# Layer 2 of a graph stack in blocks of 64 neighbours, and the hand-over to the flow layer

## The chip, the cores and the metric

The kernel runs on one core of one Trainium2 chip. The metric is the device time in microseconds, the median of several executions. All data is float32.

## The reference

Four graph layers follow each other on x of 32 batches, 512 nodes and 64 features, with one adjacency matrix adj of 512x512 for all. Each normalizes x, applies a relu, and adds its result to x:

```
for layer in (L0, L1, L2, L3):
    h = max(layernorm(x), 0)
    x = x + layer(h, adj)
L0: h @ w_self + (adj @ h) @ w_nbr + bias
L1: twice  z = relu((adj @ z) @ w_i)
L2: Wh = h @ W.T;  e = leaky_relu(e1[:, None] + e2[None, :], 0.2)
    att = softmax(e where adj > 0);  elu(att @ Wh)
L3: the flow layer: 8 heads of softmax((h_k h_k^T) * adj) @ h_k, leaky_relu,
    then one more such layer over the 8 heads put side by side
```

In layer 2, e1 and e2 are one number for each node: Wh times one half of the vector a. The change concerns layer 2, and the place where the flow layer begins.

## The kernel before

Nodes lie on the partitions, 128 at a time (C = 4 chunks). Layers 0 to 2 work on pairs of batches, M = 16 pairs, as a software pipeline. The function `slot(k)` of the stream (L837) is one turn of it: layer 0 of pair k, layer 1 of pairs k-2 and k-3, and layer 2 of pairs k-4 and k-5. The order of the calls in `slot` is the order of the instructions on TensorE (PE), VectorE (DVE) and ScalarE (ACT); each engine works through its queue in that order. There are M + 6 turns, k = 0 to 21. A few single steps stand after certain turns: weights, masks, scales, and at the end `judge_rows` and `judge`, which test whether adj has the form that the fast path needs.

Layer 2 is the class `Gat`. The softmax weight of neighbour j for node i splits into factors, so that no exponential of 512x512 is needed: a number c for each i, a number q for each neighbour j, and the weight max(c, q) times a 0/1 mask. A pair takes these steps:

- `flip` and `prepare` (turn k = pair + 4): the transposed features ht hold batch 0 of the pair on partitions 0 to 63 and batch 1 on 64 to 127. `project` with the block-diagonal weights wgT2 gives wh for both batches (L725, 4 matmuls of 128x128 with 128 columns). Four matmuls with wa2 give e2 (L747, 2 columns), and one for each batch gives e1, spread over all partitions (L753, 512 columns). ACT makes v's last column, q and c from them by exponentials.
- `weigh`: DVE scales wh by that last column.
- `scores` (turn k = pair + 5): for each batch and each chunk of 128 neighbours one DVE operation (L779) writes the weights s, 128x512.
- `values`: acc (L789) is the sum over neighbours, 4 chunks of nodes by 4 chunks of neighbours for each batch, each a matmul of a 128x128 block of s with 65 columns of v. A float32 matmul stands in the trace as two instructions, each with its weight load.
- `end`: DVE divides (L801, L802), ACT makes the exponential e of elu (L807), DVE adds to x (L810, L811) and centres x for the next normalization, ACT squares it (L813). Its variance goes into the next turn's sums (L684, L691, L699).

The mask of layer 2 is made once by one DVE operation from the transposed adjacency (L935).

The flow layer is a second schedule, `run` (L962), with a `slot(k)` of its own (L978), from k = -12. Its first unit is prepared in the first turns: DVE normalizes (L475 to L479), GpSimd scales into hs (L484), TensorE transposes into hx_ps (L291), ACT copies to hx, TensorE multiplies into g_ps (L509), ACT copies to g (L521), and then the scores s_ps (L387) begin. The PSUM buffers of this schedule (ps_s, ps_m, ps_v) take the place of those of the stream (ps_t, ps_o, ps_g), which are given back in between.

Of the kernel before, what the change touches and what calls it, by code (L numbers as in the profile page):

```python
# [22 lines left out]
def fast_form(  # L23
# [51 lines left out]
    adj_raw = setup.tile([P, C, N], F32, name="adj_raw")  # L75
# [54 lines left out]
    wgT2 = setup.tile([P, F2], F32, name="wgT2")  # L130
# [3 lines left out]
    wa2 = setup.tile([P, 2], F32, name="wa2")  # L134
# [105 lines left out]
    def gat_weights():  # L240
        pw = acc("wgT_ps", [P, F2])
        nc.tensor.transpose(pw, wg2, ident)
        nc.scalar.copy(wgT2, pw)
# [4 lines left out]
        nc.vector.memset(wa2, 0.0)  # L248
        for k in range(2):
            nc.vector.tensor_copy(wa2[halves(k), k : k + 1], wa[halves(k), 1:2])  # L250
# [207 lines left out]
    class Heads(Pair):  # L458
# [31 lines left out]
        def prep_pe(self, step):  # L490
            b, i = self.b, self.i
            if step == -1 and i == 0:
                Heads.hx[b] = pair_transpose(
                    ps_m, lambda n: wk.tile([P, N], F32, name=n), Heads.hs.pop(b), "hx",
                    nc.scalar.copy, "m",
                )
# [3 lines left out]
        def row_halves(self, off):  # L500
            b, i = self.b, self.i
            if off == -C:

                pss = [ps_m.tile([P, N], F32, name="g_ps", tag="m") for k in range(2)]
# [13 lines left out]
                for k in range(2):  # L518
                    u = self.pair[k]
                    u.g = wk.tile([P, N], F32, name="g", bufs=3)  # L520
                    nc.scalar.copy(u.g, pss[k])  # L521
# [28 lines left out]
    class Out(Pair):  # L550
# [51 lines left out]
        def end_late(self, step):  # L602
# [4 lines left out]
            elif step == 2:  # L607
                xb = row_pair("y")[:, 0].rearrange("p (k c f) -> p k c f", k=2, c=C)
                for k in range(2):
# [7 lines left out]
                    )  # L617

# [9 lines left out]
    with (  # L628
# [105 lines left out]
        class Gat:  # L734
# [8 lines left out]
            def prepare(self):  # L743
                self.wh_ps = project([(self.ht, wgT2)], "wh")
                e2 = ps_t.tile([P, C, 2], F32, name="e2_ps", tag="ps")
                for c in range(C):
                    nc.tensor.matmul(  # L747
                        e2[:, c], lhsT=self.ht[:, c * P : (c + 1) * P], rhs=wa2,
                        start=True, stop=True,
                    )  # L750
                e1 = [ps_t.tile([P, N], F32, name="e1_ps", tag="ps") for k in range(2)]
                for k in range(2):
                    nc.tensor.matmul(  # L753
                        e1[k], lhsT=wa1[halves(k), :], rhs=self.ht[halves(k), :],
                        start=True, stop=True,
                    )
                self.v = work.tile([P, 2, C, F + 1], F32, name="v")
                self.q = tiny.tile([P, C, 2], F32, name="q")
                nc.scalar.activation(
                    self.v[:, :, :, F].rearrange("p k c -> p c k"), e2, AF.Exp, scale=0.2  # L760
                )
                nc.scalar.activation(self.q, e2, AF.Exp, scale=0.8)
                self.c = row_pair("c")
                for k in range(2):
                    nc.scalar.activation(self.c[:, k], e1[k], AF.Exp, scale=-0.8)

            def weigh(self):
                nc.vector.tensor_tensor(
                    self.v[:, :, :, :F],
                    self.wh_ps.rearrange("p c k f -> p k c f"),  # L770
                    self.v[:, :, :, F : F + 1].to_broadcast([P, 2, C, F]),
                    OP.mult,
                )

            def scores(self, k):

                self.s = getattr(self, "s", []) + [[row_pair("s") for j in range(C // 2)]]
                for j in range(C):
                    nc.vector.scalar_tensor_tensor(  # L779
                        self.s[k][j // 2][:, j % 2], self.c[:, k], self.q[:, j, k : k + 1],  # L780
                        mask_t[:, j], op0=OP.max, op1=OP.mult,
                    )

            def values(self, k):
                acc = ps_g.tile([P, C, F + 1], F32, name="acc")
                self.acc = getattr(self, "acc", []) + [acc]
                for r in range(C):
                    for j in range(C):
                        nc.tensor.matmul(  # L789
                            acc[:, r],  # L790
                            lhsT=self.s[k][j // 2][:, j % 2, r * P : (r + 1) * P],
                            rhs=self.v[:, k, j],
                            start=(j == 0),
                            stop=(j == C - 1),
                        )

            def end(self):
# [8 lines left out]
                e = work.tile([P, 2, C, F], F32, name="e")  # L806
# [6 lines left out]
                nc.scalar.activation(o, o, AF.Square)  # L813

        n0, n1, n2, gat = {}, {}, {}, {}
        nt1b, z, po0 = {}, {}, {}
# [20 lines left out]
        def slot(k):  # L837
# [25 lines left out]
            u = gat.get(k - 5)  # L863
# [33 lines left out]
            if k - 6 in gat:  # L897
                some.append(gat.pop(k - 6))
# [3 lines left out]
            if u:  # L902
                u.values(0)
                u.values(1)
# [11 lines left out]
            if l1:  # L916
                nt1b[k - 2] = neighbours(lambda c: z[:, c, :])
            if u:
                u.end()

        mask_t = setup.tile([P, C, N], F32, name="mask_t")
        with tc.manual_schedule(
# [7 lines left out]
            for k in range(M + 6):  # L930
                slot(k)
                if k == 0:
                    gat_weights()
                elif k == 1:
                    nc.vector.tensor_scalar(mask_t, adj_t, 0.0, None, op0=OP.is_gt)  # L935
                elif k == 2:
                    masks()
                elif k == 3:
                    flow_weights()
                elif k == 4:  # L940
                    scales()
                elif M < k <= M + C:
                    judge_rows(k - M - 1)
                elif k == M + C + 1:
                    judge()
# [14 lines left out]


    def run(units, products):  # L962
        units = units + [None] * 4

        def at(k, off, span=C):

            for u in range(len(units)):
                if units[u] and 0 <= k - u * C - off < span:
                    yield units[u], k - u * C - off

        exps = []

        def led_in(k):
            for u, j in at(k, -3 * C, 3 * C + END + 5):
                if u.leads(j - 3 * C):
                    yield u, j - 3 * C

        def slot(k):  # L978
            for u, r in at(k, -1):
                u.scores(r)  # L980

            led = list(led_in(k))
            for u, off in led:
                u.row_halves(off)

            while exps:
                exps.pop(0)()

            copies = []

            def transposes():
                for u, j in at(k, TR):
                    copies.append(u.transpose(j))

            if not led:
                transposes()
            for u, j in at(k, VA):
                u.values(j)  # L1000
            for u, j in at(k, VA - 1, 1):
                u.make_v()
# [654 lines left out]
```

## Time and profile before

| | before |
|---|---|
| median of 3 runs | 2357.64 us (2357.25 to 2358.01) |
| profiled execution, own time | 2361.5 us |
| its span, first to last instruction | 2359.7 us |
| mean granted TensorE clock | 0.981 |
| first flow scores (s_ps) start | 480.16 us |

Layers 0 to 2 take the first fifth of the span. The page's slices are 59 us each, so they are slices 1 to 8 and a little of the ninth; the rest is the flow layer. In the timelines PE is a matmul, PEld a weight load, and a number in square brackets is the time that the engine stood idle before the row, with the instruction that ended it. Neighbouring rows of one group are merged: the length is from the start of the first to the end of the last.

### The profile page before, as it was taken

Reading aid. Unit: us, or ns where it says so; the run is one execution under the profiler, and the core shown is the slowest. Engines: PE = TensorE matmul, PEld = TensorE weight load, DVE = VectorE, ACT = ScalarE, POOL = GpSimd, SP = SyncE. Lnnn points to the kernel's source line nnn. Section 1 sums busy time; section 2 is a strip of 40 time slices with the busy share of each in tenths; the row PEclk is TensorE's granted clock in tenths of the full one; section 3 lists DMA queues with packets and bytes.
Section 4 is the critical chain, followed back from the end, with each engine's and each line's share of the span. In section 5 each row is a group of like instructions: output and inputs, shape, how many; then the busy total and the mean of one; then the engine's idle time right before and its main releaser. Section 6 shows DMA issues by size and latency. Waiting matters only on the chain.

```text
span 2359.7 us, 46961 instructions
## 1 busy us (share of the span) xinstructions
PE 2259.6 (96%) x17786; PEld 1107.3 (47%) x17786; DVE 1792.1 (76%) x4350; ACT 1583.2 (67%) x3660; POOL 68.0 (3%) x104
## 2 busy tenths in 40 slices
PE   7999999689999999999999999999999999999997
PEld 4677777634444444444444444444444444444443
DVE  5788878577777777777777777777777787878776
ACT  3444443277777777777777777777777777778775
POOL 2000000000000000000000000000000000000000
PEclk9999999589999999999999999999999999999999
DMA  3000000000000000000000000000000000000001
GB/s 106 1 1 1 1 1 1 0 15 24 20 28 21 27 24 24 28 20 28 22 26 24 24 24 24 24 24 24 24 24 26 22 29 19 24 19 24 20 24 38
DMA packets 44059, 51.89 MB, mean 22 GB/s; under 512 B 15864, under 2 KB 25248, under 8 KB 43696
## 3 DMA queue, kind: packets, MB, share of 16 engines
q1 hardware_dynamic: 43312, 48.60, 6.6%
q8 instruction: 142, 2.33, 0.4%
q0 software_dynamic: 512, 0.20, 0.1%
q14 instruction: 93, 0.76, 0.1%
HBM read 43.98 MB, written 4.78 MB: 21 GB/s over the span
## 4 chain that ended last, share of the span: by engine, by line
PE 89%; DVE 6%; POOL 2%; ACT 1%; issue 1%; DMA 1%; SPq 0%; POOLq 0%; DVEq 0%; ACTq 0%
PE s_ps L387 23%; PE av L415 22%; PE pt_ps L400 13%; PE nt_ps L706 7%; PE acc L789 6%; PE gT_ps L566 5%; PE y_ps L527 5%; PE g_ps L509 2%; DVE pt_att L408 2%; POOL hs L484 2%; PE po L725 1%; PE hx_ps L291 1%; PE e_ps L753 1%; PE po1a L725 1%; PE wh L725 1%
## 5 line engine op out<-in xcount | busy, mean ns | idle before, releaser
L366 ACT ACTIVATE p_att<-s_att,negmax 128x512 f32<-128x512 f32 x1152 | 827.6, 723 | 0.0
L373 DVE CUSTOM_DVE_ANT_0 s_att<-s_ps,flow_neg 128x512 f32<-128x512 f32 x1152 | 739.9, 680 | 5.3 <-PE s_ps L387 5.2
L408 DVE COPY pt_att<-pt_ps 128x512 f32<-128x512 f32 x576 | 395.6, 687 | 281.0 <-PE pt_ps L400 223.7
L387 PE MATMUL s_ps<-hx,g 64*128 64x512 f32 x2048 | 571.0, 636 | 5.8 <-DVE negmax L373 5.1
L415 PE MATMUL av<-pt_att,hn 128*64 128x512 f32 x2048 | 552.4, 618 | 0.0
L400 PEld LDWEIGHTS pt_ps<-ident,p_att 64*128 64x128 f32 x9216 | 373.6, 138 | 374.1 <-issue 227.7
L406 ACT COPY pt_att<-pt_ps 128x512 f32<-128x512 f32 x576 | 334.6, 581 | 156.6 <-PE pt_ps L400 150.7
L400 PE MATMUL pt_ps<-ident,p_att 64*128 64x64 f32 x9216 | 415.2, 226 | 2.3 <-ACT pt_att L406 0.8
L535 ACT ACTIVATE cat<-y_ps,bh 128x512 f32<-128x512 f32 x256 | 162.0, 684 | 168.4 <-PE y_ps L527 168.4
L387 PEld LDWEIGHTS s_ps<-hx,g 64*128 64x128 f32 x2048 | 156.5, 188 | 245.7 <-DVE negmax L373 178.3
L366 ACT ACTIVATION_READ_ACCUMULATOR p_att<-s_att,negmax 128x1 f32 x1152 | 224.5, 195 | 0.0
L444 DVE TENSOR_TENSOR o_att<-av,recb 128x512 f32<-128x512 f32 x144 | 99.6, 691 | 140.5 <-PE av L415 140.5
L415 PEld LDWEIGHTS av<-pt_att,hn 128*64 128x64 f32 x2048 | 101.4, 135 | 156.7 <-PE s_ps L387 86.4
L312 DVE SCALAR_TENSOR_TENSOR cat<-cat 128x1024 f32<-128x1024 f32 x128 | 155.6, 1215 | 0.0
L789 PE MATMUL acc<-v,s 128*128 128x65 f32 x1024 | 136.5, 301 | 10.3 <-DVE s L779 10.3
L789 PEld LDWEIGHTS acc<-v,s 128*128 128x128 f32 x1024 | 134.8, 217 | 13.5 <-issue 12.3
L527 PE MATMUL y_ps<-o_att,wh_sb 64*128 64x512 f32 x512 | 131.7, 591 | 0.0
L566 PE MATMUL gT_ps<-cat,wo_sb 128*64 128x512 f32 x512 | 131.7, 593 | 0.0
L521 ACT COPY g<-g_ps 128x512 f32<-128x512 f32 x128 | 68.7, 589 | 84.8 <-PE g_ps L509 84.8
L706 PE MATMUL nt_ps<-adj_t,hn 128*128 128x512 f32 x256 | 115.9, 596 | 0.8 <-DVE hn L670 0.8
L373 DVE DVE_READ_ACCUMULATOR2_ANT negmax<- 128x1 f32 x1152 | 95.6, 83 | 0.0
L387 PE MATMUL s_ps<-gs 64*128 64x512 f32 x256 | 72.3, 641 | 24.2 <-DVE gs L584 24.2
(169 smaller groups left out, 1603.1 us busy)
## 6 DMA issues: line engine op xcount, KB each, us to landing
recb<-rec_row SPq DMA_DIRECT2D x288, 128.0 KB
rec_row<-rect SPq DMA_DIRECT2D x576, 1.0 KB
out_dram<-y SPq DMA_DIRECT2D x32, 128.0 KB
x<-in_x_dram SPq DMA_DIRECT2D x3, 1024.0 KB
x<-in_x_dram SPq DMA_DIRECT2D x4, 256.0 KB
adj_raw<-in_adj_dram SPq DMA_DIRECT2D x1, 1024.0 KB
wh_sb<-in_L_gnn_Wh_dram SPq DMA_DIRECT2D x2, 256.0 KB
wo_sb<-in_L_gnn_W_out_dram SPq DMA_DIRECT2D x1, 256.0 KB
```

The source lines that it names most:

```text
L366: nc.scalar.activation(self.p[:, k, r, :], ns[:, k], AF.Exp, bias=self.negmax[:, k, r : r + 1], scale=-1.0, accum_out=self.sum[:, k, r : r ...
L373: nc.vector.tensor_tensor_reduce(out=ns[:, k], in0=ps[:, k], in1=flow_neg[:, r], scale=-1.0, scalar=BIG, op0=OP.add, op1=OP.min, accum_out ...
L387: nc.tensor.matmul(ps[:, k], lhsT=g[halves(k), r * P : (r + 1) * P], rhs=x[halves(k), :], start=True, stop=True,)
L400: nc.tensor.transpose(ps[half][:, k, r], self.p[halves(half), k, r, j * P : (j + 1) * P], ident[halves(half), halves(half)],)
L406: nc.scalar.copy(pth[:, :, :, 0, :], ps[0])
L408: return lambda: nc.vector.tensor_copy(pth[:, :, :, 1, :], ps[1])
L415: nc.tensor.matmul(self.av[halves(k), :], lhsT=self.v(k, j), rhs=pt[k], start=(j == 0), stop=(j == C - 1),)
L527: nc.tensor.matmul(ps, lhsT=wh_sb[halves(k), h, :], rhs=self.o[halves(k), :], start=True, stop=True,)
L535: nc.scalar.activation(self.cat[:, k], pss[k], AF.Identity, bias=bh[:, h : h + 1], scale=1.0)
L566: nc.tensor.matmul(self.gps[halves(k), :], lhsT=wo_sb[:, h, :], rhs=Heads.cat[b + k, h], start=(h == 0), stop=(h == H - 1),)
L706: nc.tensor.matmul(p, lhsT=lhs(k), rhs=adj_t[:, k, :], start=(k == 0), stop=(k == C - 1))
L789: nc.tensor.matmul(acc[:, r], lhsT=self.s[k][j // 2][:, j % 2, r * P : (r + 1) * P], rhs=self.v[:, k, j], start=(j == 0), stop=(j == C - 1),)
```

## The change

Layer 2 takes the neighbours in 8 blocks of 64 instead of 4 of 128. Both batches of a pair now share each tile: batch 0 on partitions 0 to 63, batch 1 on 64 to 127. wh and e2 come from one matmul for each block and batch, with W and its product with a side by side in wgv (65 columns); batch k uses the rows and writes the partitions of half k. c is one tile for both batches. In `values` the two batches alternate, each on its row half of TensorE, into an accumulator of its own. The mask needs both halves of the partitions for each block: four DVE operations write one half each, and four DMAs on the SP queue copy it to the other.

The last pair is scored, multiplied and ended in the turn in which it is prepared (k = 19), so there are M + 5 turns. The single steps now stand before the last part of a turn (`end`), and the judge rows come one turn earlier. The exponential e goes to a buffer of another pool. The first 11 turns of the flow schedule, up to g, run after turn k = 17 (M + 1), in the stream and with its PSUM buffers; `run` becomes `planned`, which returns its `slot`. From there on the flow schedule is as it was.

```diff
     def gat_weights():
         ...
-        nc.scalar.copy(wgT2, pw)
+        for k in range(2):
+            nc.scalar.copy(wgv[halves(k), :F], pw[halves(k), halves(k)])
         ...
-        nc.vector.memset(wa2, 0.0)
-        for k in range(2):
-            nc.vector.tensor_copy(wa2[halves(k), k : k + 1], wa[halves(k), 1:2])
+        nc.vector.tensor_copy(wgv[:, F:], wa[:, 1:2])
...
     class Gat:
             def prepare(self):
-                self.wh_ps = project([(self.ht, wgT2)], "wh")
-                e2 = ps_t.tile([P, C, 2], F32, name="e2_ps", tag="ps")
-                for c in range(C):
-                    nc.tensor.matmul(
-                        e2[:, c], lhsT=self.ht[:, c * P : (c + 1) * P], rhs=wa2,
-                        start=True, stop=True,
-                    )
-                e1 = [ps_t.tile([P, N], F32, name="e1_ps", tag="ps") for k in range(2)]
+                self.wh_ps = [
+                    ps_t.tile([P, C, F + 1], F32, name="wh_ps", tag="ps") for b in range(2)
+                ]
+                for b in range(2 * C):
+                    for k in range(2):
+                        nc.tensor.matmul(
+                            self.wh_ps[b // C][halves(k), b % C],
+                            lhsT=self.ht[halves(k), b * F : (b + 1) * F],
+                            rhs=wgv[halves(k), :], start=True, stop=True,
+                        )
+                e1 = ps_t.tile([P, N], F32, name="e1_ps", tag="ps")
                 for k in range(2):
                     nc.tensor.matmul(
-                        e1[k], lhsT=wa1[halves(k), :], rhs=self.ht[halves(k), :],
+                        e1[halves(k), :], lhsT=wa1[halves(k), :F], rhs=self.ht[halves(k), :],
                         start=True, stop=True,
                     )
...
+                for b in range(2):
+                    e2 = self.wh_ps[b][:, :, F]
+                    some = slice(b * C, (b + 1) * C)
+                    nc.scalar.activation(self.v[:, some, F], e2, AF.Exp, scale=0.2)
+                    nc.scalar.activation(self.q[:, some], e2, AF.Exp, scale=0.8)
+                self.c = row_pair("c")[:, 0]
+                nc.scalar.activation(self.c, e1, AF.Exp, scale=-0.8)
...
+            def scores(self, part):
+                self.s = getattr(self, "s", []) + [row_pair("s") for b in range(C // 2)]
+                for b in range(part * C, (part + 1) * C):
                     nc.vector.scalar_tensor_tensor(
+                        self.s[b // 2][:, b % 2], self.c, self.q[:, b : b + 1],
+                        mask_t[b // C][:, b % C], op0=OP.max, op1=OP.mult,
+                    )
...
+            def values(self):
+                self.acc = [
+                    ps_g.tile([P, C, F + 1], F32, name="acc") for k in range(2)
+                ]
                 for r in range(C):
+                    for b in range(2 * C):
+                        for k in range(2):
+                            nc.tensor.matmul(
+                                self.acc[k][:, r],
+                                lhsT=self.s[b // 2][halves(k), b % 2, r * P : (r + 1) * P],
+                                rhs=self.v[halves(k), b],
+                                start=(b == 0), stop=(b == 2 * C - 1),
+                            )
...
-                e = work.tile([P, 2, C, F], F32, name="e")
+                e = row_pair("e")[:, 0].rearrange("p (k c f) -> p k c f", k=2, c=C)
...
-        def slot(k):
+        def slot(k, more):
...
+            if more:
+                more()
+            last = gat.pop(M - 1) if k - 4 == M - 1 else None
+            if last:
+                last.scores(0)
+                last.scores(1)
             if u:
                 u.end()
+            if last:
+                last.values()
+                last.end()
...
+        def edges():
+            for b in range(2):
+                for k in range(2):
+                    blocks = mask_t[b][:, k::2]
+                    nc.vector.tensor_scalar(
+                        blocks[halves(k)], adj_t[halves(k), b * C // 2 : (b + 1) * C // 2],
+                        0.0, None, op0=OP.is_gt,
+                    )
+                    nc.sync.dma_start(blocks[halves(1 - k)], blocks[halves(k)])
...
             start()
-            for k in range(M + 6):
-                slot(k)
...
+            begun = {
+                0: gat_weights,
+                1: edges,
+                2: masks,
+                3: flow_weights,
+                4: scales,
+                M + 4: judge,
+            }
+            for c in range(C):
+                begun[M + c] = lambda c=c: judge_rows(c)
+            for k in range(M + 5):
+                slot(k, begun.get(k))
+                if k == M + 1:
+                    for i in range(-3 * C, -1):
+                        flow_slot(i)
...
+        for k in range(-1, (len(flow) + 4) * C):
+            flow_slot(k)
```

## The prediction, made before the changed kernel ran

> **What bounds the kernel now.** I read the page first: busy shares, slices, clock.
>
> ```profile
> span 2359.7 us, 46961 instructions
> ...
> PE 2259.6 (96%) x17786; PEld 1107.3 (47%) x17786; DVE 1792.1 (76%) x4350; ACT 1583.2 (67%) x3660; POOL 68.0 (3%) x104
> ...
> PEclk9999999589999999999999999999999999999999
> ```
>
> TensorE is busy 96% of the time, but the clock row has a dip at slices 8 and 9, about 400 to 490 us. That is where layers 0 to 2 end and the flow layer begins. The change touches only what stands before the first flow scores (s_ps, 480.16 us): in the built programs the instructions from s_ps on are the same on PE, DVE and ACT. So the question is when the first s_ps starts.
>
> Next the chain of waits in order of time, for one slot out of the middle:
>
> ```profile
> 121.15 7.09 PE acc L789 x64
> 128.24 1.84 PE po L725 x16
> 130.08 6.87 PE nt_ps L706 x16
> 136.95 0.44 PE ht_ps L291 x4
> 137.38 0.89 PE po1b L725 x8
> 138.28 0.44 PE ht_ps L291 x4
> 138.71 3.44 PE nt_ps L706 x8
> 142.15 0.89 PE wh L725 x8
> 143.04 0.79 PE e_ps L747 x8
> 143.83 1.06 PE e_ps L753 x4
> 144.89 1.09 PE po1a L725 x8
> ```
>
> The pieces follow without a gap: a slot is 24.83 us of TensorE and nothing else (DVE is busy 21.1 of it, ACT 10.7). A cheaper DVE or ACT step is worth nothing here; only these rows count. Last the TensorE timeline where the pairs run out (columns: start, length, instructions, idle before and its releaser):
>
> ```profile
> 404.17 12.47 PE L789 MATMUL acc<-v,s 128*128 128x65 f32 x58 [0.23 <-DVE s L779]
> 422.94 2.08 PE L725 MATMUL wh<-wgT,ht 128*128 128x128 f32 x8 [5.46 <-ACT ht L293]
> 428.46 13.92 PE L789 MATMUL acc<-v,s 128*128 128x65 f32 x64
> 452.26 14.53 PE L789 MATMUL acc<-v,s 128*128 128x65 f32 x64 [9.88 <-DVE s L779]
> 477.11 0.37 PE L223 MATMUL own_ps<-ident,own 128*1 128x128 f32 x1 [8.41 <-DVE own L221]
> 480.16 6.78 PE L387 MATMUL s_ps<-hx,g 64*128 64x512 f32 x16 [0.67 <-ACT g L521]
> ```
>
> Here TensorE waits for DVE and ACT, and an acc block takes 14 us instead of 7.1, since the granted clock is 0.50 (windows of 404 to 477 us). It does not come back during 20 us of unbroken work (422.9 to 442.4), only after the dense s_ps run.
>
> **What a half-height weight load costs.** Blocks of 64 neighbours double the matmuls of acc (512 to 1024 per layer; two instructions each), half of them on each row half. The rate is set by weight loads, so I took the load rows of the timeline:
>
> ```profile
> 96.04 4.32 PEld L789 LDWEIGHTS acc<-v,s 128*128 128x128 f32 x38
> 904.75 0.30 PEld L387 LDWEIGHTS s_ps<-hx,g 64*128 64x128 f32 x4
> 906.49 0.20 PEld L415 LDWEIGHTS av<-pt_att,hn 128*64 128x64 f32 x4
> ```
>
> acc: (4.32 - 0.192) / 37 = 0.112 us per 128-column load. s_ps, row halves: four loads of 0.188 within 0.30, so two start together and the next two about 0.11 later. A half-height load of 128 columns takes as long as a full one, and the halves load side by side. av: 64 columns, (0.20 - 0.135) = 0.065 to the second pair, half of it.
>
> **The steady slot, part by part.**
> acc: 64 pairs of instructions at 0.110 to 0.116 = 7.0 to 7.4 us against 7.09: no gain in itself.
> wh and e2 (L747): 8 + 8 full loads, 0.89 + 0.79 = 1.68, become 16 pairs of 64-column loads with 65 columns streamed: about 0.06 each = 0.96. Gain 0.7.
> e1 (L753): its two matmuls already run side by side (4 instructions of 0.43 us streaming in 1.06); they still do. 0.
> Changes of array shape: each costs about 0.2 (po1a after e1: 1.09 for a block that is 0.89 elsewhere). Before there are two in a slot (into e1, out of it), after four (wh, po1a, acc, po). Loss 0.4.
> Sum per slot: -0.35, between -0.6 and -0.1. Slots 4 to 15 are TensorE-bound: 12 x 0.35 = 4.2 us.
>
> At nothing: one c exponential less, four small ones of 128x4 for two of 128x8 on ACT (10.7 of 24.8 busy); weigh as two operations (+0.1 on DVE); both accumulators now finish together, so end's first half starts 3.5 us later and ends 0.65 later. The second scores have 2.4 us of slack before acc (342.03 against 344.47); without it, acc would stop at its first row block, which now needs all eight score blocks. The mask becomes four operations on 64 partitions, about 2.5 us for 1.22; DVE idles 3.53 us at 39.81 and absorbs it. Its four 256 KB copies wait on SP behind the x loads; DMA traffic is down to 2 GB/s by 30 us, nothing else stands in that queue until 493 us, and the mask is first read at 85 us: 45 us of cover for an estimated 5. The gat_weights step loses two copies and a memset on DVE and gains an ACT copy: 0.2 less of a 1.5 us wait.
>
> **The place where a rule of the skill speaks against it.** No row of the trace has two row halves writing into one PSUM bank: s_ps, y_ps and g_ps give each half a tile of its own, and av puts two column halves into one bank (loads 6 ns apart in the 0.20 us row). In the new wh and e1, half k reads rows k and writes partitions k of one tile. The Trainium skill, TensorEngine Tiling (Array Packing), Restrictions and Gotchas, says that different row tiles cannot access the same PSUM bank simultaneously. By that rule wh takes 32 x 0.06 = 1.9 and e1 1.9 instead of 1.0: +1.8 per slot, so 1.4 slower instead of 0.35 faster. I go by the av row: there, too, two tiles share the bank but not the partitions.
>
> **The tail, step by step** (times on the clock of before; slot k is the k-th turn of the stream).
> Slot 16: judge_rows(0) moves in front of end: +4.0 us on DVE (447.35 to 451.37 is one). The second scores end at 386.9 instead of 386.1; acc(12) still ends at about 392.4.
> Slot 17: DVE goes on at 386.9 with var, weigh, relu (3.0), judge (4.0), end (4.3: the exp table load of 1.28 no longer waits behind o, since e now has another buffer), then the flow preparation hn (1.3; before it stands at 107.8, in slot 6): 399.6. POOL makes hs (1.2): 400.4. In TensorE's queue hx_ps stands next after nt of z, which ends at 396.1: 4.3 us idle. So the clock halves here, as it did at 404.
> Slot 18: hx 0.9, copy 0.6, g_ps 1.9, two g copies on ACT to 405.2; only then, in ACT's order, nt1b (405.7) and ht (406.3). Behind them po1b (to 407.6), DVE's addition, centring and second scores (412.6), wh and e1 on TensorE (411.6). acc(13) runs 411.9 to 426.1: 9.5 later than before (416.6).
> Slot 19: end 4.3, square and ht copy 1.3, wh and e1 at half clock 4.1: acc(14) 435.8 to 449.9. Meanwhile DVE does the last pair's scores (to 446.7), so acc(15) follows without the 9.88 us wait: 449.9 to 464.0.
> Slot 20: end 4.3, square 0.7, table load 1.3, root, rstd, own, own_ps 1.3: s_ps at about 471.7, since the judge rows (4.4) and g (3.0) are out of the way. Before, acc end to s_ps was 13.4; now 7.6.
> Tail: 471.7 - 480.16 = -8.4 us; the flow preparation costs 9.5 of a gain of 18.
>
> Sum: -4.2 - 8.4 - 0.2 = -12.8, less about 0.5 for a later return of the clock: -12.3. The profiled execution (span 2359.7, own time 2361.5) gives a span of 2347.4; its own time is 3.9 over the median 2357.64. From the median: 2345.3.
>
> **Rivals.**
> A. As summed, 2345, +-6 for the sizes of the slot and of some ten tail steps: 0.70.
> B. The clock stays full in the tail. Then acc(13) ends at 416, acc(14) at 432, acc(15) at 442, s_ps at 450: 30 us instead of 8.4, 2324; a halving one slot later gives some 2335. For it: blocks at half use kept the clock in the steady slots. Against it: 4.3 us idle where 2.38 and a few stalls were enough before. 0.10.
> C. Slower: the two row halves wait for each other at the shared bank. +1.8 on 12 steady slots, the same in 16 and 17, double at half clock in 18 and 19: 1.8 x 18 = +32, so 2377. It decides from 12.5 / 18 = 0.7 us per slot on. Against it: av; for it: the rule. 0.12, from 2358 on.
> D. The flow preparation costs the tail all it gains (hs or the ACT copies later still, another 8 us): only the steady gain is left, 2353. That is also the case where the change doesn't do what it says: the last pair has no slot, but its work waits as long. 0.08.
>
> **How the numbers follow.** This kernel's runs lie within 0.03%; 0.2% (4.7 us) is what can be told from no change. Faster, below 2352.9: nearly all of A, B and a third of D: 0.82. Same: rest of D, edges of A and C: 0.06. Slower: C: 0.12. Range 2331 to 2354: A, half of B, half of D; C and the full-clock end of B stay out.
>
> **What would show it.** Steady slot about 24.5 us, acc still near 7.1, wh about 1.0 with no e2. Clock 0.50 from about 400 until shortly after s_ps. The hx_ps row with some 4 us idle before it, released by POOL hs; two acc blocks back to back of 14 us each; s_ps at about 467 on the new clock. A slot over 25 us with wh near 1.9 shows C; acc of 7 us in the tail shows B. A mask wait (DMA) before the first scores, or any difference after s_ps, would make the sum wrong in a way not foreseen.

## Result and profile after

| | before | after |
|---|---|---|
| median (seven runs each, same session) | 2360.4 us (2357.25 to 2361.58) | 2341.07 us (2338.13 to 2351.17) |
| ratio, 95% interval | | 0.9933 (0.9914 to 0.9952) |
| profiled execution, own time | 2361.5 us | 2340.76 us |
| its span | 2359.7 us | 2338.9 us |
| first acc block starts | 96.15 us | 94.47 us |
| acc(12) ends (nt of z starts) | 392.23 us | 386.66 us |
| first flow scores start | 480.16 us | 459.83 us |

(acc(i) is the acc block of pair i; there are 16.) The changed kernel is faster by 0.7%, inside the range and 4 us below the point forecast. "The tail" below is the stretch from the end of acc(12) to the start of s_ps. Of the 20.8 us that the span lost, 20.3 are gone by the first flow scores: 5.6 before acc(12) ends, 14.8 in the tail. The page of the profile after:

```profile
span 2338.9 us, 49561 instructions
...
PE 2248.0 (96%) x19066; PEld 1086.8 (46%) x19066; DVE 1794.3 (77%) x4366; ACT 1576.3 (67%) x3674; POOL 68.4 (3%) x104
...
PEclk9999999599999999999999999999999999999999
```

There are more instructions and TensorE is busy for less time; the dip in the clock row is now one slice wide instead of two. A steady turn, from the TensorE timeline of after (start, length, instructions):

```profile
143.22 7.36 PE L924 MATMUL acc<-v,s 64*128 64x65 f32 x128
150.51 0.49 PE L852 MATMUL po<-ws,ht 128*128 128x128 f32 x2
...
152.40 3.60 PE L833 MATMUL nt_ps<-adj_t,z 128*128 128x512 f32 x8
...
161.04 3.60 PE L833 MATMUL nt_ps<-adj_t,hn 128*128 128x512 f32 x8
164.57 1.15 PE L878 MATMUL wh_ps<-wgv,ht 64*64 64x65 f32 x32
165.55 1.03 PE L885 MATMUL e_ps<-ht,wa 64*64 64x512 f32 x4
166.51 1.16 PE L852 MATMUL po1a<-wl,nt 128*128 128x128 f32 x8
```

The next acc starts at 167.59: a turn of 24.37 us instead of 24.83, still without a gap. The tail, same view:

```profile
394.53 1.03 PE L290 MATMUL hx_ps<-ident,hs 128*128 128x128 f32 x4 [4.17 <-POOL hs L483]
405.28 7.71 PE L924 MATMUL acc<-v,s 64*128 64x65 f32 x128
423.12 13.92 PE L924 MATMUL acc<-v,s 64*128 64x65 f32 x128
437.85 14.43 PE L924 MATMUL acc<-v,s 64*128 64x65 f32 x128 [0.82 <-DVE rec L935]
459.00 0.37 PE L223 MATMUL own_ps<-ident,own 128*1 128x128 f32 x1 [6.72 <-DVE own L221]
459.83 4.61 PE L386 MATMUL s_ps<-hx,g 64*128 64x512 f32 x12 [0.46 <-DVE unsound L224]
```

acc(13) takes 7.71 us, the other two 14: the clock halved at the hx wait as forecast, but came back for that one block. The stretches of the tail (length, busy time of TensorE, weight loads, VectorE, ScalarE and GpSimd with instructions, granted clock):

```profile
396.00:406.00 10.00, 9.17 (x65) 5.76 (x66) 4.17 (x9) 3.72 (x11) 0.00 (x0) 0.56 0.01 2
406.00:416.00 10.00, 7.45 (x124) 7.00 (x122) 9.59 (x21) 3.50 (x4) 0.00 (x0) 0.96 0.01 2
416.00:426.00 10.00, 6.52 (x64) 4.91 (x64) 9.18 (x17) 4.30 (x10) 0.00 (x0) 0.50 0.00 0
```

The seven runs show that this is not fixed: two took 2350.2 and 2351.2 us at a mean clock of 0.980 and 0.979, the other five 2338 to 2344 at 0.985 to 0.988. One acc block more at half clock would be 7 us of the 9 to 10 that part these two from the profiled run; neither of the two has a profile, so this is an estimate.

### The profile page after: what moved, and what is told of

Its sections match the earlier page's. It is cut to its first block, busy times and chain, and to the rows that moved or that the text cites. A ratio compares the mean times of both kernels' runs of the same rounds, so it can differ in the third digit from the quotient of the medians.

```text
span 2338.9 us, 49561 instructions
## 1 busy us (share of the span) xinstructions
PE 2248.0 (96%) x19066; PEld 1086.8 (46%) x19066; DVE 1794.3 (77%) x4366; ACT 1576.3 (67%) x3674; POOL 68.4 (3%) x104
## 4 chain that ended last, share of the span: by engine, by line
PE 72%; DVE 4%; POOL 2%; issue 1%; ACT 0%; DMA 0%; SPq 0%; POOLq 0%; DVEq 0%
PE s_ps L386 23%; PE av L414 23%; PE pt_ps L399 13%; PE y_ps L526 5%; PE gT_ps L565 5%; PE g_ps L508 2%; DVE pt_att L407 2%; POOL hs L483 2%; PE hx_ps L290 1%; DVE hn L475 1%; DVE s_att L372 1%; DVE hn L474 0%; DVE gs L583 0%; PE gV_ps L576 0%; PE back_ps L449 0%
## 5 line engine op out<-in xcount | busy, mean ns | idle before, releaser
L924 PE MATMUL acc<-v,s 64*128 64x65 f32 x2048 | 132.5, 291 | 1.5 <-DVE rec L935 0.8
L924 PEld LDWEIGHTS acc<-v,s 64*128 64x128 f32 x2048 | 129.5, 206 | 6.9 <-issue 2.6
```

Of the source, the lines that this page charges most:

```text
L924: nc.tensor.matmul(self.acc[k][:, r], lhsT=self.s[b // 2][halves(k), b % 2, r * P : (r + 1) * P], rhs=self.v[halves(k), b], start=(b == 0) ...
```

## Experiments

Twelve kernels, the changed one again among them, each stand beside runs of the kernel before on the same chip. The rows come from four chips, on which the kernel before had medians of 2358.0 to 2359.2 us. The intervals are 0.07 to 0.2% of a ratio to either side, so that 2 or 3 us between two rows are not told from nothing. "Half" names the acc blocks of the tail that ran wholly or partly at half clock in the profiled execution, whose own time stands beside it.

| kernel | median us (runs) | ratio to before, 95% | profiled: us, s_ps start, half |
|---|---|---|---|
| 64-blocks only | 2355.66 (12) | 0.9984 (0.9975 to 0.9992) | 2356.11, 476.31, acc 13 14 15 |
| judge rows only | 2359.55 (22) | 0.9993 (0.9986 to 1.0) | 2352.17, 470.99, 14 15 |
| own turn for the last pair | 2336.18 (4) | 0.9908 (0.9892 to 0.9925) | 2336.63, 454.30, 15 (13 for 0.7 us) |
| no preparation in the stream | 2336.48 (4) | 0.9895 (0.9881 to 0.9909) | 2336.72, 457.09, 13 14 15 |
| after, again | 2341.97 (5) | 0.9919 (0.9906 to 0.9932) | 2338.04, 457.28, 15 |
| preparation in turns 8 to 10 | 2336.38 (4) | 0.9900 (0.9886 to 0.9914) | 2336.66, 455.84, 13 15 |
| after + dense matmuls | 2341.43 (6) | 0.9927 (0.9907 to 0.9947) | 2337.08, 458.74, 15 |
| judge rows in turns 5 to 12 | 2329.83 (4) | 0.9867 (0.9849 to 0.9885) | 2337.02, 457.02, 13 14 15 |
| tail reordered | 2333.71 (4) | 0.9896 (0.9880 to 0.9913) | 2333.37, 452.65, 14 15 |
| both | 2328.49 (4) | 0.9870 (0.9854 to 0.9887) | 2332.61, 452.97, 13 14 15 |
| both + 7 dense steps | 2325.09 (4) | 0.9854 (0.9840 to 0.9868) | 2325.00, 443.86, 15 |
| both + 16 dense steps | 2318.07 (5) | 0.9826 (0.9813 to 0.9840) | 2318.68, 437.63, none |

### The 64-blocks alone

```diff
-            for k in range(M + 5):
-                slot(k, begun.get(k))
-                if k == M + 1:
-                    for i in range(-3 * C, -1):
-                        flow_slot(i)
+            for k in range(M + 6):
+                slot(k)
+                if k in begun:
+                    begun[k]()
...
```

The lines left out take the last pair's steps out of `slot` and put the judge rows back behind `end`, in turns M + 1 to M + 4.

> Only the first half of the change: blocks of 64 neighbours, wgv, the mask in two tiles and e in a row tile, but 22 turns of the stream as before, the last pair in its own turn, the judge rows and the judge where they were, and the flow preparation after the stream. Account theory: the gain ahead of the tail comes with these parts, 1.7 us before the first acc block and 0.41 us in each of 12 turns, 6.6 us; in the tail the table load that no longer waits behind o gives some 1.3 us in each of three turns, and both accumulators ending together take back 0.6 in each: about 9 us under the kernel before. Rival (the whole gain lies in the reordered tail): within 2 us of the kernel before. Rival (the two row halves wait for each other): 20 us over it.

Measured: 3 us under before, between the theories. From its first acc block to the end of acc(12) it does gain 4.6 us (291.51 against 296.08). (Two spells of half clock in its first 86 us, which the profiles of before and after do not have, hide the start.) But its tail, from acc(12)'s end to s_ps, is 88.2 us against 87.9: all that the earlier table load should give is gone. TensorE and VectorE timelines of this kernel:

```profile
397.40 1.01 PE L924 MATMUL acc<-v,s 64*128 64x65 f32 x8 [0.48 <-DVE s L911]
...
402.27 12.92 PE L924 MATMUL acc<-v,s 64*128 64x65 f32 x112 [2.31 <-DVE s L911]
```

```profile
396.51 2.73 DVE L911 SCALAR_TENSOR_TENSOR s<-c,q,mask 128x512 f32<-128x512 f32 x4
...
401.48 2.73 DVE L911 SCALAR_TENSOR_TENSOR s<-c,q,mask 128x512 f32<-128x512 f32 x4
```

acc(13) stops in its first row block for the second half of the scores (begun at 401.48), and the clock halves at 399.4. The scores end 4.9 us earlier than before (404.2 against 409.1), the block only 1.5 (415.2 against 416.6). With blocks of 128 neighbours the first batch of the pair could be multiplied before the scores of the second were there; blocks of 64 need all eight scores in each block of rows.

### The judge rows alone

```diff
+            if more:
+                more()               # judge_rows(k - M), ahead of u.end()
             if u:
                 u.end()
...
-                elif M < k <= M + C:
-                    judge_rows(k - M - 1)
```

> The kernel before, with one edit: each of the four judge rows comes a turn earlier and ahead of end instead of behind it, as in the changed kernel; blocks of 128 neighbours, the last pair's own turn and the flow preparation after the stream stay. Theory (the place of the judge rows carries what the tail gains: 4.0 us of VectorE leave the way from end to the next scores and the way to own_ps, which is what 64-block half alone, 2355.7, lacks to 2336.2): 13 to 19 us under the kernel before, 2340 to 2345. Rival (the place of the rows helps only with blocks of 64 or with the clock that came back by chance): within 6 us of the kernel before.

Measured: no difference in the median. The runs fall into two groups: 16 at 2359.0 to 2362.0 us with clock 0.980 or 0.981, and 6 at 2352.2 to 2353.3 with 0.985. The profiled one is of the second group:

```profile
405.59 7.36 PE L789 MATMUL acc<-v,s 128*128 128x65 f32 x64
...
425.91 13.92 PE L789 MATMUL acc<-v,s 128*128 128x65 f32 x64
...
445.69 14.53 PE L789 MATMUL acc<-v,s 128*128 128x65 f32 x64 [5.87 <-ACT o L813]
```

acc(13) met the full clock, and 7 us is what one acc block at half clock costs. The rival holds for the median: the moved rows pay nothing in most runs. That the slower group had acc(13) at half clock is likely from its mean clock, but none of it was profiled.

### The last pair in a turn of its own

```diff
-            last = gat.pop(M - 1) if k - 4 == M - 1 else None
-            if last:
-                last.scores(0)
-                last.scores(1)
             if u:
                 u.end()
-            if last:
-                last.values()
-                last.end()
...
-                if k == M + 1:
-                    for i in range(-3 * C, -1):
-                        flow_slot(i)
```

> The changed kernel without the preparation in the stream (2336.5 in the run before) and with the last pair in a turn of its own again; the judge rows stay where the change puts them. It stands between the 64-block half alone (2355.7) and 2336.5, and tells what the merged last turn is worth by itself. Account theory: the last acc block waits again for end of the pair ahead of it (4.3 us) and its own eight scores (5.4 us), 9 us instead of 0.8: about 2345, so the merged turn gives 9 and the place of the judge rows the other 10. Rival (the place of the judge rows does it all): 2339 or less. Rival (the merged turn does it all): 2353 or more.

The last lines take the preparation out of the stream as well. Measured: 2336.18, as fast as the kernel without preparation that merges the last turn (2336.48). The merge shows no gain, though the two profiles met different clocks, and the rival that the judge rows do it all holds: 19.5 us below the 64-blocks alone. Its timelines, TensorE and VectorE:

```profile
398.11 7.90 PE L924 MATMUL acc<-v,s 64*128 64x65 f32 x128
...
416.04 7.36 PE L924 MATMUL acc<-v,s 64*128 64x65 f32 x128
428.60 15.48 PE L924 MATMUL acc<-v,s 64*128 64x65 f32 x128 [5.20 <-ACT o L947]
```

```profile
384.17 0.42 DVE L195 TENSOR_SCALAR edge<-adj_p 128x512 f32<-128x512 f32 x1
...
388.19 0.17 DVE L935 RECIPROCAL rec<-acc 128x4 f32<-128x4 f32 x1
...
397.43 2.73 DVE L911 SCALAR_TENSOR_TENSOR s<-c,q,mask 128x512 f32<-128x512 f32 x4
```

A judge row stands in the time in which VectorE would wait for acc(12) (384.2 to 388.2, acc ends at 387.2), instead of between end and the scores; the second scores of pair 13 start at 397.43 instead of 401.48, acc(13) runs unbroken, at full clock from 398.8 on, and ends at 406 instead of 415. From there the clock does the rest: acc(14) and acc(15) with the wait between them take 416.04 to 444.08, 28.0 us, where the 64-blocks alone took 40.1 (424.48 to 464.61). In that kernel both ran at half clock and here only acc(15), so part of the 19.5 us is the clock; how much of it the place of the rows would give at one clock was not measured.

### No preparation in the stream, and the changed kernel again

```diff
-                if k == M + 1:
-                    for i in range(-3 * C, -1):
-                        flow_slot(i)
...
-        for k in range(-1, (len(flow) + 4) * C):
+        for k in range(-3 * C, (len(flow) + 4) * C):
```

> The changed kernel, but the first flow unit is not prepared in the stream: it comes after the stream, as before. Account theory (the preparation delays acc of the third last pair by the wait for hs, hx, g and the ACT copies): that block starts some 6 us earlier, and hx and g find room in the wait before own_ps; 3 to 7 us under the changed kernel if the clock behaves alike, so 2334 to 2338. Rival (the preparation is worth having, because it takes hx and g off the way to s_ps): 3 us or more over the changed kernel. Rival (the clock decides): the time goes with the granted clock of the tail, not with the waits, and the seven or so runs fall into clusters some 9 us apart.

> The changed kernel once more, on the same chip as the other two, to place it against the kernels that leave the preparation out (2336.2 to 2336.5). If the preparation in the stream costs the 5 us that separate runs suggest: 2339 to 2345, above every one of those runs. If the difference was the chip or the day: 2335 to 2338.

Measured: 2336.48 without it; the changed kernel came out at 2341.97, all five of its runs above every one of the four (on another chip, with the kernel before at 2359.2 there and 2358.9 here). The preparation in the stream costs about 5 us. The timeline without it:

```profile
400.71 8.67 PE L924 MATMUL acc<-v,s 64*128 64x65 f32 x100 [0.22 <-DVE s L911]
...
418.66 13.92 PE L924 MATMUL acc<-v,s 64*128 64x65 f32 x128
433.40 14.43 PE L924 MATMUL acc<-v,s 64*128 64x65 f32 x128 [0.82 <-DVE rec L935]
448.81 1.09 PE L290 MATMUL hx_ps<-ident,hs 128*128 128x128 f32 x4 [0.98 <-DVE o L936]
```

acc(13) starts 8 us earlier (397.31) and ends at 409.3 instead of 413.0, although the clock halved in it; hx and g lie in the wait before own_ps. acc(14) and acc(15) take 418.66 to 447.83 here, 29.2 us with no wait between them, against the 28.0 with the wait of 5.2 in the kernel above. So the merge takes out a wait, but in this execution it got both blocks at half clock.

### The preparation earlier

```diff
-                if k == M + 1:
-                    for i in range(-3 * C, -1):
-                        flow_slot(i)
+                for i in {8: range(-12, -5), 9: range(-5, -4), 10: range(-4, -1)}.get(k, ()):
+                    flow_slot(i)
```

> The changed kernel with the preparation of the first flow unit moved from the tail to turns 8, 9 and 10 of the stream: hn and hs in 8, hx in 9, g in 10. It costs about 1.9 us of TensorE there, which is the bound, and takes the wait of 4.2 us for hs, hx, the wait for its copy and g (6.5 us in all) out of the tail. Account theory: 2 to 5 us under the changed kernel, 2336 to 2339, if the clock of the tail stays as it is. Rival (the third last acc block then meets the half clock, since the wait that leads up to it goes on elsewhere): within 2 us of 2341 or slower.

Measured: 2336.38, as expected, and the same as without preparation. acc(12) ends at 388.13, 1.5 later than in the changed kernel; the tail is 5.5 us shorter (67.7 against 73.2). In the profiled run acc(13) did meet the half clock, as the rival has it, but acc(14) had the full one.

### Dense matmuls in the waits of the changed kernel

```diff
+        def warm(n):
+            p = ps_o.tile([P, N], F32, name="warm", tag="po")
+            for j in range(n):
+                nc.tensor.matmul(
+                    p, lhsT=ident, rhs=adj_t[:, j % C, :], start=(j == 0), stop=(j == n - 1)
+                )
...
```

> The changed kernel with 18 extra matmuls of 128x128 by 512 that nothing reads: 5 before hx_ps, 6 before wh of the second last pair, 7 before own_ps, each group put where TensorE waited 4 to 7 us for others. Clock theory (TensorE's half clock in the tail is what the two last acc blocks of 14 us cost): the clock stays full up to s_ps, the acc blocks take 7.3 us, s_ps comes about 14 us earlier, 2327 in all, and the runs lie within 2 us of each other. Rival (the clock in the tail is not the limit, the chain through VectorE and ScalarE is): within 2 us of the changed kernel's 2341. Rival (the extra work is in the way): slower than 2341.

Measured: the median did not move, and the runs spread over 16 us, with the clock: 2333.85 at 0.993, 2349.78 at 0.986. The clock theory as put failed. The profiled run shows why full clock in two of the blocks did not help more:

```profile
423.83 5.80 PE L924 MATMUL acc<-v,s 64*128 64x65 f32 x100 [0.22 <-DVE s L911]
435.12 14.43 PE L924 MATMUL acc<-v,s 64*128 64x65 f32 x128 [5.49 <-DVE rec L935]
```

acc(14) is done at 429.6, 7.4 us earlier than in after (9.9 if counted from the end of acc(12), which came 2.5 us later in this execution). But VectorE still has a judge row and the last eight scores ahead of end, until 434.3, so acc(15) waits 5.5 us, meets the half clock again and starts only 2.7 us earlier. VectorE had to come first.

### Less VectorE in the tail, and another order

In the first kernel the judge rows are cut in two and put into turns 5 to 12 (its lines shift by 6); in a second kernel two steps are moved; a third has both edits. The first two:

```diff
-            for c in range(C):
-                begun[M + c] = lambda c=c: judge_rows(c)
+            for c in range(2 * C):
+                begun[5 + c] = lambda c=c: judge_rows(c // 2, c % 2)
...
```

```diff
+            if k == M + 2:           # ahead of end of pair 13
+                gat[M - 1] = Gat(M - 1, n2.pop(M - 1).h)
+                gat[M - 1].flip()
+                gat[M - 2].scores(0)
+                gat[M - 2].scores(1)
...
```

> The changed kernel without the preparation in the stream, with the four judge rows (4.0 us of VectorE each) cut in halves of 2 us and put into turns 5 to 12, where VectorE waits some 4.4 us a turn. Theory (in the tail TensorE waits for VectorE, and that wait brings the half clock): the scores of the third last pair come 4 us sooner, its acc block is done at 405 instead of 410 us, 1 to 4 us less in all, 2333 to 2336. Rival (the order of the tail, not the load of VectorE, sets its end: the rows stand in waits for acc): within 1 us of 2336.5. Rival (TensorE-bound turns lose by it): slower than 2336.5 by up to 2.

> The changed kernel without the preparation in the stream, with two steps moved: the transposition of the last pair's input, and the scores of the second last pair, come ahead of end of the third last pair instead of behind it. Theory (the second last acc block waits for end of the block before it only by the order on ScalarE and VectorE): the wait of 4.6 us for ht goes and acc follows wh at once; s_ps 9 us sooner, about 2328 at half clock, less where the clock stays full. Rival (VectorE is the limit whatever the order, since it has judge, end and scores to do between two acc blocks): within 3 us of 2336.5.

> Both of the last two kernels' edits: judge rows in turns 5 to 12, and the last pair's transposition and the second last pair's scores ahead of end of the third last pair. Theory (with neither the order nor VectorE in the way TensorE has hardly a wait, so its clock stays full up to the last acc block): from the end of the third last acc block to s_ps 27 to 30 us instead of 47, about 2315. Rival (the clock drops all the same): the gain of the order alone and 2 us more, about 2326.

Measured: 2329.83, 2333.71 and 2328.49 (all three without preparation in the stream). Judge rows out of the tail gave more than expected in the median, but with runs of 2322.62 at clock 0.992 and 2337.02 at 0.985, and the slowest is the profiled one; the order gave 2.8, its rival's figure and not clear of noise; both gave 8 and stand near the rival's 2326, the clock having dropped all the same. In the reordered kernel the wait for ht is 0.73 us instead of 4.6, and VectorE is late next:

```profile
412.16 14.43 PE L924 MATMUL acc<-v,s 64*128 64x65 f32 x128 [3.64 <-DVE rec L935]
```

### The clock held

The kernel with both edits gets dense steps in its own short waits: first 7, then, in a second kernel, 16.

```diff
             if last:
+                warm(1)              # second kernel: warm(6)
                 last.values()
...
-                M + 4: judge,
+                M + 4: lambda: (warm(4), judge()),      # second kernel only
```

The other six steps are 2 ahead of po1b and 3 ahead of acc(13) in turn 18, and 1 ahead of wh in turn 19.

> The kernel with judge rows in turns 5 to 12 and the reordered tail (2328.5), plus 7 dense matmul steps of 128x128 by 512 that nothing reads (0.86 us each at full clock): 2 ahead of po1b and 3 ahead of acc of the third last pair, 1 ahead of wh and 1 ahead of the very last acc block, where TensorE waited 1.6, 1.2, 0.7 and 0.8 us. Clock theory (a few short waits are enough to halve the clock at about 399 us, and the halved clock then costs 7 us in each of the last two acc blocks): the clock stays full until after the last acc block, s_ps about 13 us earlier, 2315. Rival (the clock drops in spite of it, since blocks of 65 columns use half the array at most): 2327 to 2331. Rival (VectorE is the limit behind it): 2322 to 2326.

> The kernel at 2325.1 with more of the dense matmuls that nothing reads: 6 instead of 1 ahead of the very last acc block, where TensorE still waited 4.3 us for VectorE and the clock halved, and 4 between that block and hx. Clock theory (each acc block at half clock costs 7.1 us, and this is the last one left): that block takes 7.3 us instead of 14.4, s_ps comes 7 us earlier and its first twelve matmuls take 2.6 us instead of 4.9: 2316 to 2319. Rival (the last block was off the path that sets the end, or the clock drops all the same): within 2 us of 2325.

Measured: 2325.09, then 2318.07. In the first, acc(15) still waited 4.27 us and took 14.43; VectorE was late. In the second, the TensorE timeline and the stretches of the tail:

```profile
396.91 7.36 PE L930 MATMUL acc<-v,s 64*128 64x65 f32 x128
...
407.59 7.36 PE L930 MATMUL acc<-v,s 64*128 64x65 f32 x128
414.88 5.42 PE L982 MATMUL warm<-adj_t,ident 128*128 128x512 f32 x12
420.26 7.88 PE L930 MATMUL acc<-v,s 64*128 64x65 f32 x128
...
437.63 4.58 PE L392 MATMUL s_ps<-hx,g 64*128 64x512 f32 x12 [0.46 <-DVE unsound L230]
```

```profile
406.00:416.00 10.00, 10.00 (x163) 8.64 (x160) 6.82 (x15) 4.87 (x10) 0.00 (x0) 1.00 0.01 2
416.00:426.00 10.00, 9.86 (x107) 7.08 (x105) 7.52 (x15) 2.54 (x3) 0.00 (x0) 1.00 0.01 2
426.00:436.00 10.00, 7.52 (x54) 4.15 (x51) 5.33 (x11) 3.40 (x5) 0.00 (x0) 1.00 0.00 0
```

acc(15) starts at the same time in both (420.16 and 420.26); only its clock differs, 14.43 against 7.88 us, 6.55 of the 7.0 us that the second kernel gains in the median: the price of one block at half clock, measured. The four steps behind it gained nothing: from acc(15)'s end to s_ps it is 9.5 us, against 9.3. The clock then halved at 437.8, as s_ps began, and its first twelve instructions took 4.58 us, not the 2.6 expected. All five runs lie within 1.4 us. This kernel beats both the kernel before (0.9826) and the changed one; it spends 16 steps of TensorE on nothing but its clock.

## Why the prediction was right, and where its steps were not

**Steady slot, forecast -0.35, measured -0.46.** From the start of one row to the start of the next: wh and e2 1.77 to 0.98, -0.79 (forecast -0.7); e1 1.06 to 0.96, -0.10 (0); acc 7.10 to 7.29, +0.19 (0); into wh +0.09, po1a to acc +0.09, po +0.05. The sum is -0.47. The rows of before, to set beside those of after:

```profile
141.99 1.05 PE L725 MATMUL wh<-wgT,ht 128*128 128x128 f32 x8
142.88 0.95 PE L747 MATMUL e_ps<-wa,ht 128*128 128x2 f32 x8
143.76 1.13 PE L753 MATMUL e_ps<-ht,wa 64*128 64x512 f32 x4
144.82 1.16 PE L725 MATMUL po1a<-wl,nt 128*128 128x128 f32 x8
145.81 7.26 PE L789 MATMUL acc<-v,s 128*128 128x65 f32 x64
```

The mis-sized term is the change of array shape: forecast +0.4 for the two additional ones; the rows around the changes together lost 0.23 (with acc's own 0.19, 0.42). The forecast's own terms, -0.72 and +0.4, make -0.32 and not -0.35, so 3.8 us for twelve slots and not 4.2. Measured, twelve slots gave 4.9 us (284.09 us from acc(0) to acc(12) instead of 288.98), the last ones less than the middle ones, since acc there waits 0.22 for a score.

**The rule of the skill that spoke against the change.** The two row halves do not wait for each other at the bank. wh's 32 weight loads, two halves of one tile (weight-load timeline of after):

```profile
375.53 1.01 PEld L878 LDWEIGHTS wh_ps<-wgv,ht 64*64 64x64 f32 x32
```

32 in 1.01 us is 0.06 for each pair; in turn they would have needed 1.9 (an estimate, from 0.06 us for one load). The Trainium skill, TensorEngine Tiling (Array Packing), Restrictions and Gotchas, says that different row tiles cannot access one bank simultaneously; with each half on its own partitions, the trace shows no such wait. The measurement decides, and going by the av row was right. Rival C is out.

**At nothing.** The mask's four VectorE operations took 2.84 us (forecast 2.5), its copies no visible wait. The cover named for the second scores, 2.4 us of slack, was 1.7 in the middle turns, which is enough. In the tail of the 64-blocks alone it was missing, with the consequence that the prediction names (acc stops in its first row block), at a price of about 3.4 us in acc(13). In the changed kernel the row of acc(13) shows no stop.

**Ahead of the first acc block, forecast -0.2, measured -1.68.** One pair of profiles cannot show this size: in the twelve profiled executions of kernels with 64-blocks that block starts between 93.77 and 96.96 us. Six of those profiles show a spell of half clock below 86 us.

**The tail, forecast -8.4, measured -14.8** (from the end of acc(12), or -13.8 from its start). Step by step, forecast times less the 6.6 us by which acc(12) came early against measured: hn done 393.0, 393.2; hs 393.8, 394.5; hx waits 4.3, 4.17, and the clock halves there; acc(13) starts at 405.3, 405.28. The order of the steps and every wait up to here were right. Then acc(13) was to take 14.2 us at half clock and took 7.71. That is the step that failed, 6.5 of the error of 8.5 us against the profiled span (2347.4 forecast, 2338.9 measured); the early part makes 1.5, the steady turns 0.7, and small terms of both signs cancel. From acc(13)'s end on the forecast holds again: acc(14) starts 10.1 us later (9.7 forecast), acc(15) follows 0.82 behind it, and from its end to s_ps it is 7.55 (7.6). The table load did leave the way behind o, as forecast.

The reason for the failed step was "it does not come back during 20 us of unbroken work", read from one execution of before. Part of that reading holds: acc(14) ran 13.92 us at half clock without a break, and the clock did not come back. The Trainium skill, TensorE: Matmul & The Clock Gate, Part 1, would have it back after one busy window of about 3.4 us, and these blocks do not agree. What the reading missed is the work between the blocks.

The granted clock shows what brought it back. In all fourteen traces it changes only at moments that lie a whole number of steps of 3.41 us apart: after lost it at 394.66, had it back three steps later at 404.90, and lost it again at 415.14. Here are single steps of after (columns as above):

```profile
401.48:404.90 3.42, 3.42 (x39) 2.29 (x38) 2.72 (x6) 0.39 (x1) 0.00 (x0) 0.50 0.02 5
404.90:408.31 3.41, 3.28 (x50) 2.77 (x50) 3.41 (x7) 2.38 (x7) 0.00 (x0) 1.00 0.00 0
...
418.55:421.96 3.41, 2.48 (x34) 2.02 (x36) 3.41 (x6) 1.35 (x6) 0.00 (x0) 0.50 0.00 0
421.96:425.38 3.42, 3.42 (x26) 2.27 (x22) 2.83 (x6) 2.12 (x3) 0.00 (x0) 0.50 0.00 0
```

and of the second profile of the same kernel, ahead of its acc(14):

```profile
418.94:422.36 3.42, 2.91 (x36) 2.02 (x36) 3.42 (x6) 0.93 (x5) 0.00 (x0) 0.50 0.00 0
422.36:425.77 3.41, 3.41 (x56) 3.02 (x56) 3.02 (x8) 2.85 (x4) 0.00 (x0) 1.00 0.00 0
```

At half clock, wh (L878) and e1 (L885) together take about as long as one step. In the kernels with 64-blocks, where most of both fell into one half-clock step (19 or more of the 32 instructions of wh, and at least the first two of the four of e1 done at its end), the clock was full from the next step on, seven times out of seven. Where the step ended before the first two of e1 were done, it stayed at half, five times out of five. After a half-clock step filled by acc alone it stayed at half 84 times out of 84, in all traces. In after the edge at 421.96 came 0.4 us before the first two of e1 ended; in the second profile it came at 422.36, just behind them, and acc(14) took 7.36 us instead of 13.92. So the clock of a block hung on where the steps happened to lie in that execution, and one execution of before could not tell. These are readings of traces: no run moved wh and e1 against the steps on purpose, and what in them counts was not separated.

**How much was luck.** The forecast started from a median of three runs (2357.64); with seven that median is 2360.4. The change itself was forecast at -12.3 us and measured at -15.8 by the ratio, -19.3 by the medians. The extra gain is mostly the one block at full clock, which not every run had: the two runs at 2350 and 2351 lie above the point about as far as the median lies below it. The sign and the waits were earned by the working; that the median came within 4.2 us of the point is in part luck.

**"The flow preparation costs 9.5 of a gain of 18."** The sign was right and the size twice too large: it costs about 5. Without it acc(13) did start 8 us earlier, but met the half clock in its middle. The gain of 18 was put down in part to the wrong edit. The wait of 9.88 us before acc(15) is indeed gone, but without the preparation, giving the last pair its turn back changes nothing that the runs tell (2336.18 against 2336.48). What carries the tail is that the judge rows stand in VectorE's wait for acc, and only together with the 64-blocks: the rows alone give 0 in the median, the 64-blocks alone 3, both (with the last pair's own turn) 22. Shown is that they do not add up, and that the profiles differ in how many acc blocks met the half clock; how much of the joint gain would remain at one fixed clock was not measured.

**Rivals.** B happened in part: the clock came back for one block in the profiled run. Its full form, forecast at 2324, was seen in no run of the changed kernel; 2318 was reached by another kernel, with the tail reordered and the clock held on purpose. D did not happen; the preparation takes 5, not all.

## What to carry to other kernels

Where TensorE runs out of work at the hand-over between two stages, count the blocks that will run at half clock before counting the waits: a removed wait is worth little if the next block runs at half clock, and a wait of 4 us can cost 7 more behind it. Put work that nobody waits for (here four checks of 4 us on VectorE) where its engine waits anyway. If edits are to be judged there, look at the granted clock of every run: two kernels can differ by 7 us because one block met another clock.

## What the runs showed of the hardware

Not expected: the granted clock in the tail varies from run to run of one kernel. The judge-rows kernel shows two groups 7 us apart, with clock 0.985 and 0.981. In each trace the clock changes only at steps of 3.41 us, and the steps lie differently in each execution: in the two profiles of the changed kernel they are 0.4 us apart against the work.

Blocks of 65 columns never brought the clock back (84 full steps at half clock), and in the turns of 24 us, without waits, they never lost it. Waits lose it, and short ones are enough: in the 64-blocks alone there were 1.58, 0.48 and twice 0.22 us in the 8 us before the clock halved.

Dense matmuls in the waits, 16 steps of about 0.9 us, held the clock at full in the profiled run until s_ps began. All five runs have a mean clock of 0.997 or 0.998 and lie within 1.4 us, where the changed kernel's first seven spread over 13.
